# Channels 128 to 255 of both streams by taps summed in PSUM, b*s on GpSimd, a new bank plan, and W of f behind the projections

## The chip, the core and the metric

The kernel runs on one core of one Trainium2 chip. A core has five engines with a queue each: TensorE (PE in the profile; PEld is its weight load), VectorE (DVE), ScalarE (ACT), GpSimd (POOL) and SyncE (SP, which here only starts DMAs). They run side by side and wait for each other by semaphores. PE writes its results to PSUM, eight banks of 2 KB per partition, from where VectorE and ScalarE read them. The metric is the time of the whole program on the device in microseconds; the kernel before took 2464.41 us, the median of three runs (2457.53 to 2467.1).

## What is computed

A block of a vision network on `x` (4, 128, 96, 96): group normalisation, then a gated scan over the pixels in four directions (rows forward and backward, columns forward and backward), a fusing 1x1 convolution, and the residual.

```python
t = _grouped1x1(x, in_proj_w, in_proj_b, G)            # 4 groups
u, gate = (t[:, :HID], t[:, HID:])                     # 256 channels each
u = jax.nn.silu(u)
u = lax.conv_general_dilated(u, dw_w, ...)             # depthwise, K = 5
s = _conv1x1(u, ssm_in_w)                              # 32 channels
a = DMIN + (DMAX - DMIN) * jax.nn.sigmoid(_conv1x1(u, ssm_delta_w, ssm_delta_b))
a = jnp.clip(a, 0.0001, 0.9999)
bb = jnp.tanh(_conv1x1(u, ssm_b_w, ssm_b_b))
cc = jnp.tanh(_conv1x1(u, ssm_c_w, ssm_c_b))
prefix = jnp.cumsum(jnp.log(a), axis=-1)
hst = jnp.exp(prefix) * jnp.cumsum(bb * s * jnp.exp(-prefix), axis=-1)
u = u + _conv1x1(cc * hst + ssm_d[None, :, None] * s, ssm_out_w)
u = _grouped1x1(u * jax.nn.sigmoid(gate), mix_w, mix_b, G)
return _conv1x1(u, out_proj_w, out_proj_b)
...
seq_all = jnp.concatenate([seq_h, seq_h[:, :, ::-1], seq_v, seq_v[:, :, ::-1]], axis=0)
...
return jnp.einsum('oc,bchw->bohw', fuse_w, y) + fuse_b[None, :, None, None]
...
x = x + _L0_conv_ref(_gn(x), ...)
```

The recurrence behind `hst` is h = a * h + b * s, a scan over 9216 positions. mix, out_proj and fuse are linear and follow each other, so the kernel multiplies them into one matrix `w_fin` ("W") per direction at the start.

## The kernel before

**Tiling.** For each of four images there are two phases: the two column directions (order V), then the two row directions (order H). In a phase a forward stream f (s = 0) and a reversed stream r (s = 1) run together. A sequence is cut into 6 steps, and a step into 4 units by the position's remainder p modulo 4, each of N = 384 positions. A *unit* is one step, p and stream; a *pair* is the units of f and r with the same step and p. There are 192 pairs. `pair(t)` (line 507) is called for t = 0 to 198 and is a software pipeline: at call t the convolution and the projections are those of pair t, the inputs ("front") those of pair t + 4, and the gate, the sum and W ("back") those of pair t - 6 (LAG). So the first six calls have no back and the last seven no projections.

**Stages of a pair**, with the names used below:
- *rows* (line 323), twice a pair, the first and the second: 8 matmuls of 32x32 tiles for one front unit and 8 for the gate of one back unit; ScalarE takes the gate through tanh (`gv`) and the front through silu (`sil`), from four banks.
- *convolution* (`conv`, line 396): the depthwise convolution of a half of the channels of a unit as 8 matmuls with a band matrix, copied to `u` by ScalarE (line 402). Of the four halves of a pair (f and r, channels 0 to 127 and 128 to 255) three are done so. The fourth, channels 128 to 255 of f, is done by *taps* (line 407): one ScalarE operation for tap 0 and four VectorE operations that add tap k, on 384 elements in SBUF.
- *projections* (`proj`, line 422): 16 matmuls of `u` with `w_proj` into two banks, giving b and a in one, c and s in the other; ScalarE evacuates c and s. `inputs` (line 443), called in the next pair, evacuates b and a through tanh (line 447), brings a into its range on GpSimd (450, 451) and multiplies b by s on VectorE, straight from PSUM (452).
- *scan* (line 454): one VectorE scan over half a step, in the first two pairs of each step. *outputs* (line 469): three GpSimd operations that make c * h + d * s.
- *ssm_out* (line 381): 16 matmuls of 32x32 tiles into four banks; VectorE adds `u` to them and multiplies by the gate, once per stream (393, 394).
- *W of f, W of r* (`accumulate`, line 475): 8 matmuls with `w_fin` and one VectorE addition of the result y to the image `acc` (490, 495, 497). W of r is issued one pair later than W of f. In the last half of an H phase finished parts go out by DMA.

In phases V, VectorE also collects the statistics of the next image (`stats_chunk`, line 310).

**What sets the order.** The loop over `pair(t)` is recorded under a manual schedule: each of PE, VectorE, ScalarE and GpSimd runs its operations in the order of the calls in `pair`, and the framework adds the waits for data and for buffers, PSUM banks among them. The bank plan is thus a plan of waits:

```python
    GATE, FRONT, CONV_R, Y_F, SMALL = (0, 1), (2, 3), (0, 1), 2, 3
    SSM, PROJ, Y_R, CONV_F = (4, 6), (5, 4), 6, 7
```

On PE a pair is: first rows, W of r (of the pair before), convolution of f, second rows, ssm_out, two convolutions of r, W of f, projections. Every matmul but those of the preparation has line 314, that of the helper `mm`, and is told apart by its tiles: `psum<-x_in,wn` rows, `psum<-sil,band` convolution, `psum<-u,w_proj` projections, `psum<-t,w_so` ssm_out, `psum<-gv,w_fin` W. The profile counts two records for each matmul of fp32.

## Time and profile before

| | |
|---|---|
| median of three runs | 2464.41 us (2457.53 to 2467.1) |
| the profiled execution | 2462.79 us, span 2461.1 us |
| granted TensorE clock, mean | 0.992 |
| matmuls of rows, busy | 389.9 us |
| matmuls of ssm_out, busy | 256.2 us |
| matmuls of the projections, busy | 533.0 us |
| matmuls of W, busy | 582.9 us |
| VectorE waiting for PE ahead of L393 | 247.5 us, 133 times |
| ScalarE waiting for PE ahead of L402 | 339.3 us, 572 times |
| GpSimd waiting for ScalarE ahead of L450 | 1190.2 us, 189 times |

The span goes from the first to the last instruction. Busy times of a group count each moment once, though up to 16 small matmuls run at the same time. A row of the groups reads: line, engine, operation, what is written and what is read, shape and count, then busy us and the mean ns of one, then the idle time of the engine just before it and what ended that. A row of the timeline reads: start, length, engine, line, operation, and in brackets the idle time ahead of it.

### The profile page before, as it was taken

What the parts mean: (1) busy time and instruction counts of PE and PEld (TensorE: products, weight loads), DVE (VectorE), ACT (ScalarE), POOL (GpSimd) and SP (SyncE); (2) the same over time, 40 slices, a digit from 0 to 9 for tenths busy, and PEclk for the clock granted to TensorE, in tenths of its full rate; (3) what the DMA queues carried; (4) which work ended last, traced back from release to release, by engine and by line L of the source; (5) the groups of instructions that cost most, each with busy time, mean ns of one, the idle gap of its engine ahead of it and who ended that gap; (6) DMA issues with size and microseconds to landing.
All of it is one profiled execution on the core that took longest, in us unless ns stands there. A gap on an engine that the chain in (4) does not pass through costs nothing.

```text
span 2461.1 us, 89876 instructions
## 1 busy us (share of the span) xinstructions
PE 2389.1 (97%) x40016; PEld 913.3 (37%) x40016; DVE 1859.2 (76%) x2343; ACT 1572.8 (64%) x2912; POOL 1051.3 (43%) x1170
## 2 busy tenths in 40 slices
PE   6999999999999999999999999999999999999997
PEld 3333333333333333333333333333333333333331
DVE  3688777777887787777877788777777777777774
ACT  4666676666666666666665666666666666666641
POOL 4344444444444444444443444444443444444441
PEclk9999999999999999999999999999999999999997
DMA  5212111113332211111342211111232111111111
GB/s 140 56 47 54 47 41 32 38 31 89 98 100 52 54 44 34 35 38 31 93 139 55 54 46 41 31 38 31 52 120 89 31 38 33 38 31 38 25 45 56
DMA packets 79283, 134.21 MB, mean 55 GB/s; under 512 B 11440, under 2 KB 73392, under 8 KB 78896
## 3 DMA queue, kind: packets, MB, share of 16 engines
q1 hardware_dynamic: 76704, 127.64, 19.3%
q8 instruction: 314, 5.14, 0.9%
q10 hardware_dynamic: 2192, 0.83, 0.1%
q14 instruction: 73, 0.60, 0.1%
HBM read 109.55 MB, written 18.87 MB: 52 GB/s over the span
## 4 chain that ended last, share of the span: by engine, by line
PE 82%; DVE 9%; POOL 3%; ACT 3%; issue 1%; DMA 0%; DVEq 0%; SPq 0%
PE psum L314 82%; DVE t L465 4%; ACT t L447 2%; DVE gv L394 2%; DVE psum L393 2%; POOL t L450 1%; POOL t L451 1%; DVE u L415 0%; DMA out<-acc 0%; DVE bn L310 0%; DMA acc<-in_xr 0%; ACT gv L353 0%; ACT L364 0%; ACT L438 0%; ACT sil L364 0%
## 5 line engine op out<-in xcount | busy, mean ns | idle before, releaser
L314 PE MATMUL psum<-sil,band 128*32 128x384 f32 x9216 | 821.6, 488 | 0.0
L450 POOL TENSOR_SCALAR t<-t 64x384 f32<-64x384 f32 x192 | 186.3, 970 | 1190.4 <-ACT t L447 1190.2
L314 PE MATMUL psum<-gv,w_fin 128*32 128x384 f32 x6144 | 582.9, 497 | 31.0 <-DVE gv L394 29.0
L393 DVE TENSOR_TENSOR psum<-psum,u 128x768 f32<-128x768 f32 x384 | 369.3, 962 | 248.3 <-PE psum L314 247.5
L314 PE MATMUL psum<-u,w_proj 128*32 128x384 f32 x6144 | 533.0, 486 | 0.0
L415 DVE SCALAR_TENSOR_TENSOR u<-sil,w_tap,u 128x384 f32<-128x384 f32 x768 | 478.9, 624 | 56.9 <-ACT u L413 35.7
L353 ACT ACTIVATE gv<-psum,bnorm 128x384 f32<-128x384 f32 x768 | 403.7, 577 | 153.2 <-PE psum L314 153.2
L402 ACT COPY u<-psum 128x384 f32<-128x384 f32 x576 | 276.0, 479 | 339.3 <-PE psum L314 339.3
L314 PEld LDWEIGHTS psum<-sil,band 128*32 128x32 f32 x9216 | 284.0, 109 | 489.7 <-issue 344.9
L314 PE MATMUL psum<-x_in,wn 32*32 32x385 f32 (+1 forms) x12288 | 389.9, 502 | 13.3 <-DVE acc L490 8.5
L394 DVE SCALAR_TENSOR_TENSOR gv<-gv,psum 128x768 f32<-128x768 f32 x384 | 366.5, 955 | 43.7 <-ACT sil L364 0.9
L314 PEld LDWEIGHTS psum<-gv,w_fin 128*32 128x32 f32 x6144 | 183.5, 110 | 388.7 <-issue 289.6
L364 ACT ACTIVATE sil<-psum,bsilu 128x385 f32<-128x385 f32 x576 | 314.6, 586 | 5.6 <-PE psum L314 5.4
L438 ACT ACTIVATE t<-psum,b_proj 64x384 f32<-64x384 f32 x192 | 110.6, 576 | 321.7 <-PE psum L314 263.8
L314 PEld LDWEIGHTS psum<-u,w_proj 128*32 128x32 f32 x6144 | 211.9, 110 | 280.2 <-issue 276.6
L472 POOL TENSOR_TENSOR t<-t,t 64x384 f32<-64x384 f32 x192 | 289.1, 1506 | 15.0
L471 POOL TENSOR_TENSOR t<-t,t 64x384 f32<-64x384 f32 x192 | 249.5, 1300 | 95.9 <-DVE t L465 85.9
L314 PE MATMUL psum<-t,w_so 32*32 32x384 f32 x6144 | 256.2, 493 | 2.9 <-DVE t L452 2.9
L452 DVE TENSOR_TENSOR t<-psum,t 64x384 f32<-64x384 f32 x192 | 179.4, 934 | 103.9 <-ACT t L447 103.0
L447 ACT ACTIVATE t<-psum,b_proj 128x384 f32<-128x384 f32 x192 | 208.6, 1087 | 25.3 <-PE psum L314 2.3
L314 PEld LDWEIGHTS psum<-x_in,wn 32*32 32x32 f32 x12288 | 99.3, 104 | 275.3 <-ACT sil L364 129.9
L451 POOL TENSOR_SCALAR t<-t 64x384 f32<-64x384 f32 x192 | 184.9, 963 | 15.9
(62 smaller groups left out, 1166.5 us busy)
## 6 DMA issues: line engine op xcount, KB each, us to landing
x_in<-in_xs SPq DMA_DIRECT2D x96, 385.0 KB, 4.4
x_in<-in_xs SPq DMA_DIRECT2D x384, 96.2 KB, 2.6
out<-acc SPq DMA_DIRECT2D x24, 768.0 KB, 4.9
xs<-in_xr SPq DMA_DIRECT2D x72, 192.0 KB, 2.4
acc<-in_xr SPq DMA_DIRECT2D x18, 768.0 KB, 4.9
acc<-in_xr SPq DMA_DIRECT2D x24, 192.0 KB, 3.6
w_fuse<-in_fuse_wT ACTq DMA_DIRECT2D x1, 256.0 KB, 4.8
w_proj<-in_proj_wT ACTq DMA_DIRECT2D x1, 128.0 KB
```

Source lines behind the costliest of these rows:

```text
L314: nc.tensor.matmul(o[r, : rhs.shape[-1]], lhsT, rhs, start=start, stop=stop, skip_group_check=True)
L353: nc.scalar.activation(gv[:, j, :], bank(GATE[j])[:, :N], AF.Tanh, bias=gbn[:, 2 + j : 3 + j], scale=0.5,)
L364: nc.scalar.activation(sil[:, j, g, :], bank(front_banks[j])[:, : N + 1], AF.Silu, bias=bn[:, j : j + 1] if by_taps(s, j) else bsil[:, j, ...
L393: nc.vector.tensor_add(pz, pz, bu["u"])
L394: nc.vector.scalar_tensor_tensor(gv, gv, 1.0, pz, ALU.add, ALU.mult)
L402: nc.scalar.copy(un["u"][:, j, :], pc[:, :N])
L415: nc.vector.scalar_tensor_tensor(part, src, w_tap[:, k : k + 1], part, ALU.mult, ALU.add)
L447: nc.scalar.activation(ta[:, p, :], bank(PROJ[0])[:, :N], AF.Tanh, bias=b_proj[:, 0:1])
L450: nc.gpsimd.tensor_scalar(a, a, half, DMIN + half, ALU.mult, ALU.add)
L451: nc.gpsimd.tensor_scalar(a, a, 0.9999, 0.0001, ALU.min, ALU.max)
L471: nc.gpsimd.tensor_mul(ta[64:P, p, :], tb[0:64, p, :], ta[0:64, p, :])
L472: nc.gpsimd.tensor_add(tb[64:P, p, :], ta[64:P, p, :], tb[64:P, p, :])
```

## The change

Channels 128 to 255 are now done by taps for both streams. `u`, `sil` and the taps cover f and r in one operation of 2 x 384 elements; the partial sum stands in two PSUM banks (`TAPS`, 6 and 7), and only the last tap writes `u`. The band matrix keeps half of its columns. The addition of `u` behind ssm_out is one operation over four banks instead of two over two banks each. The four results of the projections are evacuated by ScalarE right behind them; s goes to a new tile `s` in SBUF, from where GpSimd multiplies b by it. `inputs` is gone. W of f stands behind the projections, taps 0 to 2 between the convolution of r and the projections, and taps 3 and 4 behind the first rows of the next pair. All banks are assigned anew: `rows` is told its banks (FIRST and SECOND), ssm_out uses 0 to 3, W of both streams bank 0, the convolutions 1 and 4, the projections 5 and 4.

On PE, between ssm_out and the next rows, the program before has (`sil_1` is the silu of stream r; `gv` goes into W; the rows of `w_proj` alternate 16 times between the two streams):

```order
L314 MATMUL psum<-t_18_10689,w_so 32x384 x16
L314 MATMUL psum<-sil_1_10861,band 32x384 x16
L314 MATMUL psum<-gv_0_1_0_11612,w_fin 32x384 x8
L314 MATMUL psum<-u_1_3_0_11568,w_proj 32x384
L314 MATMUL psum<-u_1_3_1_11682,w_proj 32x384
```

and the changed one, from the same place to the first rows (`x_in`) of the next pair, behind whose 16 alternating rows comes W of r:

```order
L315 MATMUL psum<-t_18_9965,w_so 32x384 x16
L315 MATMUL psum<-sil_9863,band 32x384 x8
L315 MATMUL psum<-u_1_3_0_10799,w_proj 32x384 x16
L315 MATMUL psum<-gv_0_1_0_10852,w_fin 32x384 x8
L315 MATMUL psum<-x_in_68,wn_3587 32x385
L315 MATMUL psum<-x_in_68,wn_3587 32x384
```

Eight of the 16 convolution matmuls are gone there, and W of f has moved behind the projections, next to the rows and W of r.

On VectorE, a pair with neither scan half, whose back is in a phase H and whose own convolution in a phase V (`bn` are statistics, `acc<-psum,b_fin` the y of f, `acc<-psum` that of r, `u` written from `sil` a tap), before:

```order
L495 SCALAR_TENSOR_TENSOR acc<-psum,b_fin,acc 128x16x24
L415 SCALAR_TENSOR_TENSOR u_0_2_0_14307<-sil_0_13458,w_tap,u_0_2_0_14307 128x384 x4
L452 TENSOR_TENSOR t_24_14163<-psum,t_24_14163 64x384
L497 TENSOR_TENSOR acc<-psum,acc 128x16x24
L310 BN_STATS bn_14085<-xs_2_14381 128x6
L393 TENSOR_TENSOR psum<-psum,u_5_0_0_13430 128x2x384
L394 SCALAR_TENSOR_TENSOR gv_5_0_0_14352<-gv_5_0_0_14352,psum 128x768
L393 TENSOR_TENSOR psum<-psum,u_5_0_1_13545 128x2x384
L394 SCALAR_TENSOR_TENSOR gv_5_0_1_14400<-gv_5_0_1_14400,psum 128x768
L495 SCALAR_TENSOR_TENSOR acc<-psum,b_fin,acc 128x16x24
```

and the changed one:

```order
L497 SCALAR_TENSOR_TENSOR acc<-psum,b_fin,acc 128x16x24
L419 SCALAR_TENSOR_TENSOR psum<-sil_12578,w_tap,psum 128x2x384
L419 SCALAR_TENSOR_TENSOR u_0_2_0_13361<-sil_12578,w_tap,psum 128x2x384
L499 TENSOR_TENSOR acc<-psum,acc 128x16x24
L311 BN_STATS bn_13170<-xs_2_13447 128x6
L387 TENSOR_TENSOR psum<-psum,u_5_0_0_12541 128x4x384
L389 SCALAR_TENSOR_TENSOR gv_5_0_0_13416<-gv_5_0_0_13416,psum 128x768
L389 SCALAR_TENSOR_TENSOR gv_5_0_1_13466<-gv_5_0_1_13466,psum 128x768
L419 SCALAR_TENSOR_TENSOR psum<-sil_12578,w_tap,psum 128x2x384 x2
L497 SCALAR_TENSOR_TENSOR acc<-psum,b_fin,acc 128x16x24
```

The product of L452 is gone, the four taps are split around the y of f, two behind the products with the gate and two ahead of the y of r, and the two adds of L393 are one (L387).

On ScalarE, the end of a pair and the start of the next (`t` are the tiles of the scan: the first holds b and a, the other c and d * s), before:

```order
L402 COPY u_1_2_1_18543<-psum 128x384 x2
L413 ACTIVATE u_1_3_0_18571<-sil_0_17561,w_tap 128x384
L438 ACTIVATE t_31_18291<-psum,b_proj 64x384
L441 ACTIVATE t_31_18291<-psum,d_sb 64x384
L447 ACTIVATE t_31_18290<-psum,b_proj 128x384
L353 ACTIVATE gv_0_1_0_18615<-psum,bnorm_10976 128x384 x2
```

and the changed one:

```order
L403 COPY u_4_3_0_12406<-psum 128x384
L417 ACTIVATE psum<-sil_12039,w_tap 128x2x384
L445 ACTIVATE t_22_12140<-psum,b_proj 128x384
L446 ACTIVATE t_22_12141<-psum,b_proj 64x384
L448 COPY s_12563<-psum 64x384
L449 ACTIVATE t_22_12141<-psum,d_sb 64x384
L349 ACTIVATE gv_3_2_0_12595<-psum,bnorm_3722 128x384 x2
```

The tanh of b and a (L447, now L445) is the first of the evacuations, the copy of s is new, and one convolution copy is gone.

The diff, without the preparation on the host and the parts that only follow the new shapes:

```diff
-    GATE, FRONT, CONV_R, Y_F, SMALL = (0, 1), (2, 3), (0, 1), 2, 3
-    SSM, PROJ, Y_R, CONV_F = (4, 6), (5, 4), 6, 7
+    FIRST = ((2, 3), (1, 5))
+    Y_R, CONV_F = 0, 1
+    SECOND = ((6, 7), (4, 5))
+    SSM = 0
+    CONV_R, PROJ, TAPS, Y_F, SMALL = 4, (5, 4), 6, 0, 5
...
-    band = wp.tile([P, 2, R, 2, 4, 32], F32, name="band")
+    band = wp.tile([P, R, 2, 4, 32], F32, name="band")
...
     sils = {}
 
-    def rows(i, bi, front_banks=FRONT):
+    def rows(i, bi, banks):
...
-            if g == 0:
-                sils[step, s] = wk.tile(
-                    [P, 2, 4, N + 1], F32, tag=f"sil{s}", name=f"sil_{step}_{s}"
-                )
-            sil = sils[step, s]
+            if k == 0:
+                sils[step] = wk.tile([P, 2, 2, 4, N + 1], F32, tag="sil", name=f"sil_{step}")
+            sil = sils[step][:, s]
...
                     r = slice(32 * j, 32 * j + 32)
-                    m, q = (c, g) if by_taps(s, j) else (g, c)
-                    mm(bank(front_banks[j]), c, wn[r, 32 * m : 32 * m + 32], x_in[s][r, q, :],
+                    m, q = (c, g) if j else (g, c)
+                    mm(bank(banks[0][j]), c, wn[r, 32 * m : 32 * m + 32], x_in[s][r, q, :],
                        True, True)
                 if bi is not None:
                     r = slice(64 + 32 * j, 96 + 32 * j)
-                    mm(bank(GATE[j]), c, gwn[r, 32 * c : 32 * c + 32],
+                    mm(bank(banks[1][j]), c, gwn[r, 32 * c : 32 * c + 32],
...
     def ssm_out(bi):
 
-        pair = units[bi], units[bi + 1]
+        pair = units[bi : bi + 2]
...
                     r = slice(64 * j + 32 * s, 64 * j + 32 * s + 32)
-                    mm(bank(SSM[s] + j), c, w_so[r, 128 * j + 32 * c : 128 * j + 32 * c + 32],
+                    mm(bank(SSM + 2 * s + j), c, w_so[r, 128 * j + 32 * c : 128 * j + 32 * c + 32],
                        z[r, p, :], True, True)
+        pz = psum[:, SSM : SSM + 4, :N]
+        nc.vector.tensor_add(pz, pz, us[bi].rearrange("p s j n -> p (s j) n"))
         for s, bu in enumerate(pair):
-            pz, gv = psum[:, SSM[s] : SSM[s] + 2, :N], bu["v"]
-            nc.vector.tensor_add(pz, pz, bu["u"])
-            nc.vector.scalar_tensor_tensor(gv, gv, 1.0, pz, ALU.add, ALU.mult)
-
-    def conv(un, j):
-        sil = sils[un["step"], un["s"]]
-        pc = bank(CONV_R[j] if un["s"] else CONV_F)
+            nc.vector.scalar_tensor_tensor(
+                bu["v"], bu["v"], 1.0, pz[:, 2 * s : 2 * s + 2, :], ALU.add, ALU.mult
+            )
+
+    us = {}
+
+    def conv(i, s):
+
+        un = units[i]
+        sil = sils[un["step"]][:, s]
+        pc = bank(CONV_R if s else CONV_F)
         for k in range(2):
             for g in range(4):
-                mm(pc, g, band[:, j, un["p"], k, g, :], sil[:, j, g, k : k + N], k == 0, k == 1)
-        nc.scalar.copy(un["u"][:, j, :], pc[:, :N])
-
-    def new_u(un):
-        un["u"] = wk.tile([P, 2, N], F32, tag="u", bufs=2 * LAG + 2, name=f"u_{un['id']}")
-
-    def taps(un, ks):
-        sil, j = sils[un["step"], un["s"]], 1
+                mm(pc, g, band[:, un["p"], k, g, :], sil[:, 0, g, k : k + N], k == 0, k == 1)
+        nc.scalar.copy(us[i][:, s, 0, :], pc[:, :N])
+
+    def new_u(i):
+        us[i] = wk.tile([P, 2, 2, N], F32, tag="u", bufs=LAG + 1, name=f"u_{units[i]['id']}")
+
+    def taps(i, ks):
+
+        un = units[i]
+        sil = sils[un["step"]][:, :, 1]
+        part = psum[:, TAPS : TAPS + 2, :N]
         for k in ks:
             off, q = divmod(un["p"] + k, R)
-            src, part = sil[:, j, q, off : off + N], un["u"][:, j, :]
+            src = sil[:, :, q, off : off + N]
             if k == 0:
                 nc.scalar.activation(part, src, AF.Copy, scale=w_tap[:, 0:1])
             else:
                 nc.vector.scalar_tensor_tensor(
-                    part, src, w_tap[:, k : k + 1], part, ALU.mult, ALU.add
+                    us[i][:, :, 1, :] if k == K - 1 else part,
+                    src,
+                    w_tap[:, k : k + 1],
+                    part,
+                    ALU.mult,
+                    ALU.add,
                 )
...
-    def proj(i, which):
-
-        un = units[i]
-        step, p = un["step"], un["p"]
+    def proj(i):
+
+        step, p = units[i]["step"], units[i]["p"]
...
-        pp = bank(PROJ[which])
-        cols = (qb, qb, qa, qa) if which == 0 else (qc, qc, qs, qs)
-        for j in range(2):
-            for c in range(4):
-                mm(pp, c, w_proj[:, j, cols[c]], units[i + c % 2]["u"][:, j, :], j == 0, j == 1)
-        if which == 1:
-            nc.scalar.activation(
-                tb[0:64, p, :], pp[0:64, :N], AF.Tanh, bias=b_proj[0:64, 1:2]
-            )
-            nc.scalar.activation(tb[64:P, p, :], pp[64:P, :N], AF.Copy, scale=d_sb[64:P, :])
-
-    def inputs(i):
-
-        un = units[i]
-        ta, p = scans[un["step"]][0], un["p"]
-        nc.scalar.activation(ta[:, p, :], bank(PROJ[0])[:, :N], AF.Tanh, bias=b_proj[:, 0:1])
+        for j in (1, 0):
+            for bk, cols in zip(PROJ, ((qb, qb, qa, qa), (qc, qc, qs, qs))):
+                for c in range(4):
+                    mm(bank(bk), c, w_proj[:, j, cols[c]], us[i][:, c % 2, j, :], j == 1, j == 0)
+        pa, pb = (bank(bk)[:, :N] for bk in PROJ)
+        nc.scalar.activation(ta[:, p, :], pa, AF.Tanh, bias=b_proj[:, 0:1])
+        nc.scalar.activation(tb[0:64, p, :], pb[0:64, :], AF.Tanh, bias=b_proj[0:64, 1:2])
+        st = wk.tile([P, N], F32, tag="s", name=f"s_{i}")
+        nc.scalar.copy(st[0:64, :], pb[64:P, :])
+        nc.scalar.activation(tb[64:P, p, :], pb[64:P, :], AF.Copy, scale=d_sb[64:P, :])
         a = ta[64:P, p, :]
         half = (DMAX - DMIN) / 2
         nc.gpsimd.tensor_scalar(a, a, half, DMIN + half, ALU.mult, ALU.add)
         nc.gpsimd.tensor_scalar(a, a, 0.9999, 0.0001, ALU.min, ALU.max)
-        nc.vector.tensor_mul(ta[0:64, p, :], bank(PROJ[1])[64:P, :N], ta[0:64, p, :])
...
         conv_here = i < NU
         front = i + UB if i + UB < NU else None
-        back = 0 <= bi < NU
-        if 0 <= i - 2 < NU:
-            inputs(i - 2)
-        rows(front, bi if back else None)
+        back = bi if 0 <= bi < NU else None
+        rows(front, back, FIRST)
+        if conv_here and i:
+            taps(i, range(3, K))
         if 0 <= bi - 2 < NU:
             accumulate(units[bi - 1])
         if conv_here:
-            conv(units[i], 0)
+            conv(i, 0)
         if k < 2 and 0 <= t // R - 1 < NU // UB:
             scan(t // R - 1, k)
...
-            rows(None if front is None else front + 1, bi + 1 if back else None)
-        if back:
+        if front is not None or back is not None:
+            rows(None if front is None else front + 1, None if back is None else bi + 1, SECOND)
+        if back is not None:
             ssm_out(bi)
         if conv_here:
-            new_u(units[i + 1])
-            for j in range(2):
-                conv(units[i + 1], j)
-        if back:
+            conv(i, 1)
+        if i + 2 < NU:
+            new_u(i + 2)
+            taps(i + 2, range(3))
+        if conv_here:
+            proj(i)
+        if back is not None:
             accumulate(units[bi])
         if later:
             next(later[0], None)
-        if i + 2 < NU:
-            new_u(units[i + 2])
-            taps(units[i + 2], range(K))
-        if conv_here:
-            proj(i, 1)
-            proj(i, 0)
 
     for _ in stats_finish(b0):
         pass
     for i in range(UB):
-        rows(i, None, (2 * (i % 2), 2 * (i % 2) + 1))
-    new_u(units[0])
-    taps(units[0], range(K))
+        rows(i, None, (SECOND[0] if i % 2 else FIRST[0], None))
+    new_u(0)
```

43 lines of the change are left out of this document (20 added, 23 removed).

## The prediction

> **The bound.** I read the page first: the busy shares and the chain that ended last.
>
> ```profile
> PE 2389.1 (97%) x40016; PEld 913.3 (37%) x40016; DVE 1859.2 (76%) x2343; ACT 1572.8 (64%) x2912; POOL 1051.3 (43%) x1170
> PE 82%; DVE 9%; POOL 3%; ACT 3%; issue 1%; DMA 0%; DVEq 0%; SPq 0%
> ```
>
> TensorE is busy 97% of the span and carries 82% of the chain; the next engine, VectorE, is at 76%. Busy shares are averages, so the second view is the table by stage. I cut it where the first pair with all its stages begins (t = 6) and where the last pair with projections ends; 186 pairs lie between.
>
> ```profile
> 100.24:2392.06 2291.82, 2261.64 (x38565) 862.76 (x38562) 1781.08 (x2228) 1507.13 (x2786) 991.98 (x1038) 1.00 0.20 52
> ...
> 2394.00:2419.00 25.00, 16.18 (x248) 4.73 (x240) 16.95 (x18) 5.40 (x11) 15.61 (x16) 0.86 0.22 79
> 2419.00:2461.00 42.00, 30.18 (x320) 8.16 (x320) 17.90 (x23) 6.31 (x12) 1.43 (x2) 0.68 0.10 39
> ```
>
> The columns are the stretch, its length, then busy time on PE, PEld, DVE, ACT and POOL, and the granted clock (the third number from the end). A pair takes 2291.82 / 186 = 12.32 us, PE is busy 98.7% of it at a clock of 1.00, and 2461.1 - 2291.8 = 169.3 us lie outside. So a pair of the middle decides, and the third view is the timeline of one in which nothing waits:
>
> ```profile
> 1147.53 0.94 PE L314 MATMUL psum<-x_in,wn 32*32 32x385 f32 x32
> 1148.40 1.50 PE L314 MATMUL psum<-gv,w_fin 128*32 128x384 f32 x16
> 1149.72 1.48 PE L314 MATMUL psum<-sil,band 128*32 128x384 f32 x16
> 1151.12 0.94 PE L314 MATMUL psum<-x_in,wn 32*32 32x385 f32 x32
> 1151.79 1.30 PE L314 MATMUL psum<-t,w_so 32*32 32x384 f32 x32
> 1153.03 2.79 PE L314 MATMUL psum<-sil,band 128*32 128x384 f32 x32
> 1155.63 1.48 PE L314 MATMUL psum<-gv,w_fin 128*32 128x384 f32 x16
> 1156.92 2.77 PE L314 MATMUL psum<-u,w_proj 128*32 128x384 f32 x32
> 1159.62 0.94 PE L314 MATMUL psum<-x_in,wn 32*32 32x385 f32 x32
> ```
>
> Starts are in the first column. From start to start: first rows 0.87, W of r 1.32, convolution of f 1.40, second rows 0.67, ssm_out 1.24, convolutions of r 2.60, W of f 1.29, projections 2.70; together 12.09. The mean of 12.32 is these steps plus 0.23 of waits. VectorE in the same pair:
>
> ```profile
> 1149.97 0.56 DVE L497 TENSOR_TENSOR acc<-psum,acc 128x384 f32<-128x384 f32 x1 [0.23 <-PE psum L314]
> 1153.05 0.97 DVE L393 TENSOR_TENSOR psum<-psum,u 128x768 f32<-128x768 f32 x1 [2.53 <-PE psum L314]
> 1154.13 0.95 DVE L394 SCALAR_TENSOR_TENSOR gv<-gv,psum 128x768 f32<-128x768 f32 x1
> 1155.00 0.96 DVE L393 TENSOR_TENSOR psum<-psum,u 128x768 f32<-128x768 f32 x1
> 1156.07 0.95 DVE L394 SCALAR_TENSOR_TENSOR gv<-gv,psum 128x768 f32<-128x768 f32 x1
> 1157.25 0.62 DVE L495 SCALAR_TENSOR_TENSOR acc<-psum,b_fin,acc 128x384 f32<-128x384 f32 x1 [0.23 <-PE psum L314]
> ```
>
> VectorE waits for PE here, not the reverse. The rows also give the latencies I need: an add of y starts 1.57 after W of r starts and 1.62 after W of f; the add behind ssm_out starts 1.26 after ssm_out; an operation that needs the result before it starts 0.11 after its end (1153.05 + 0.97, then 1154.13), and one that doesn't starts 0.87 after the start of one of 768 elements.
>
> **TensorE.**
>
> ```profile
> L314 PE MATMUL psum<-sil,band 128*32 128x384 f32 x9216 | 821.6, 488 | 0.0
> ```
>
> Three convolutions a pair become two. Of the 2.60 for the two of r one half goes: 1.30 a pair (a third of the group's 821.6 us is 274; 192 x 1.30 = 250). The other steps stay, in another order, so PE's steps are 12.09 - 1.30 = 10.79. That alone would be 186 x 10.79 + 169 = 2176 us; what follows is what is late next.
>
> **New banks.** Three places now share a bank that did not before, and each wait is a small sum of rows.
>
> ```profile
> 1151.26 0.48 ACT L402 COPY u<-psum 128x384 f32<-128x384 f32 x1 [0.59 <-PE psum L314]
> ```
>
> ```profile
> 1118.27 0.95 DVE L394 SCALAR_TENSOR_TENSOR gv<-gv,psum 128x768 f32<-128x768 f32 x1
> ```
>
> ```profile
> 1119.37 1.50 PE L314 MATMUL psum<-gv,w_fin 128*32 128x384 f32 x16 [0.27 <-DVE gv L394]
> ```
>
> The copy out of a convolution starts 1.54 after it (1149.72, 1151.26) and takes 0.48; PE starts 0.15 after the release (1119.22, 1119.37).
> - W of f and, in the next pair, W of r both use bank 0. W of r needs the add of f's y done: 1.62 + 0.62 + 0.15 = 2.39 after W of f starts. PE gets there after 1.40 + 0.87 = 2.27 (W of f now stands ahead of rows, like the convolution with its 1.40). Wait: 0.12. Behind it stand on PE the convolution of f and all else of the pair.
> - ssm_out writes bank 1, from which f's convolution is copied: 1.54 + 0.48 + 0.15 = 2.17 against 1.40 + 0.67. Wait: 0.10.
> - The projections write bank 4, from which r's convolution is copied, after one quarter of their work in bank 5: 2.17 against 1.30 + 0.64. Wait: 0.23.
>
> Together 0.45, so 11.24 a pair, if VectorE keeps up.
>
> **VectorE.** Its operations and their durations:
>
> ```profile
> L415 DVE SCALAR_TENSOR_TENSOR u<-sil,w_tap,u 128x384 f32<-128x384 f32 x768 | 478.9, 624 | 56.9 <-ACT u L413 35.7 <-ACT sil L364 1.0
> L393 DVE TENSOR_TENSOR psum<-psum,u 128x768 f32<-128x768 f32 x384 | 369.3, 962 | 248.3 <-PE psum L314 247.5
> L394 DVE SCALAR_TENSOR_TENSOR gv<-gv,psum 128x768 f32<-128x768 f32 x384 | 366.5, 955 | 43.7 <-ACT sil L364 0.9 <-ACT u L402 0.5
> L452 DVE TENSOR_TENSOR t<-psum,t 64x384 f32<-64x384 f32 x192 | 179.4, 934 | 103.9 <-ACT t L447 103.0
> L465 DVE TENSOR_TENSOR_SCAN t<-t,t 64x768 f32<-64x768 f32 x40 | 116.8, 2919 | 14.9 <-POOL t L451 14.9
> L465 DVE TENSOR_TENSOR_SCAN t<-t 64x768 f32<-64x768 f32 x56 | 107.4, 1918 | 5.2 <-POOL t L451 3.6
> ```
>
> Four taps of 384 elements become four of 768, with the sum in PSUM. The trace has no such tap. It can't be shorter than the 384 form (0.62) nor should it pass two of them (1.25); the nearest row is L394, the same operation on 768 elements with one operand in PSUM: I take 0.96. The two adds of L393 become one of 1536: between 0.97 and 1.92; the step from L497 (0.56 at 384) to L393 (0.96 at 768) is 0.40 per 384, so 0.96 + 0.81 = 1.77. The product of L452 (0.93) goes to GpSimd. A pair therefore gains 4 x 0.96 + 1.77 - 4 x 0.62 - 2 x 0.96 - 0.93 = 0.28 on VectorE: 9.7 (1859.2 / 192) becomes 10.0, of 11.2. The sum fits; the order is the question, because f's y, which now gates bank 0, stands behind two taps. From the start of ssm_out: 1.26, the add 1.77, 0.11, two products at 0.87, the first of two taps 1.07 (0.96 + 0.11) and the second 0.88, so VectorE is free for f's add at 6.83. It is due at 1.24 + 1.30 + 0.23 + 2.58 (projections: twice the 1.29 of W of f, whose operations are half as many) + 1.62 = 6.97. That is a slack of 0.14, so no wait in a pair without a scan.
>
> The scan stands between the add of r's y and the add behind ssm_out, in two pairs of four. Before it come f's add, taps three and four and r's add. F's add starts 1.62 after W of f, the third tap 0.53 later (0.09 before its end, as above), the fourth 1.07, r's add 0.87: 4.09, which is 1.70 after W of r (2.39), where r's y alone would let it start after 1.57. The first scan (2.92 in 40 of 48 steps) then ends at 1.70 + 0.47 + 2.92 = 5.09 after W of r; the add behind ssm_out is due at 1.32 + 1.40 + 0.67 + 0.10 + 1.26 = 4.75. Late by 0.34, less the slack: 0.20. The second (1.92) ends by 4.09, in time.
>
> ```profile
> L310 DVE BATCH_NORM_STATS2 bn<-xs 128x6 f32<-128x384 f32 x72 | 39.9, 555 | 1.1
> ```
>
> In 72 of 192 pairs L310 adds 0.47 there: 0.67 in such a first scan pair; the second still ends by 4.56. Over four pairs 0.62 x 0.20 + 0.38 x 0.67 = 0.38, that is 0.09 a pair: 11.33 a pair.
>
> **Other engines.** ScalarE loses one convolution copy (0.48), gains a copy of s (0.48), and its tap of 384 (0.62) becomes one of 768, at most 1.24: from 8.2 (1572.8 / 192) to 8.8 of 11.33. Its chain behind r's convolution, 1.24 + 1.54 + 0.48 + 1.24 = 4.50 after ssm_out starts, is done before VectorE comes to the first tap (1.26 + 1.77 + 0.11 + 0.87 + 0.87 = 4.88), even at that bound.
>
> ```profile
> L471 POOL TENSOR_TENSOR t<-t,t 64x384 f32<-64x384 f32 x192 | 249.5, 1300 | 95.9 <-DVE t L465 85.9
> L450 POOL TENSOR_SCALAR t<-t 64x384 f32<-64x384 f32 x192 | 186.3, 970 | 1190.4 <-ACT t L447 1190.2
> L451 POOL TENSOR_SCALAR t<-t 64x384 f32<-64x384 f32 x192 | 184.9, 963 | 15.9
> ```
>
> ```profile
> L447 ACT ACTIVATE t<-psum,b_proj 128x384 f32<-128x384 f32 x192 | 208.6, 1087 | 25.3 <-PE psum L314 2.3
> ```
>
> GpSimd's b*s is like L471 (one strided operand, strided result): 1.30, between the 0.96 of L451, with one operand, and two of L471; so 5.5 (1051.3 / 192) becomes 6.8. What it could hold up is the first scan. The tanh of L447 now comes right behind the projections and ends about 0.6 after W of f starts; then 0.97 + 0.96 + 1.30 and three gaps of some 0.1 make 4.1. The scan's turn on VectorE is at 2.39 + 1.70 + 0.47 = 4.6. Hidden, with 0.5 to spare; beyond that each first scan goes later by the excess, at 2.60 by 0.8, which is 0.2 a pair or 37 us.
>
> **Outside.** Outside the 186 pairs, the first six pairs save at most 6 x 1.30; I take 2, because taps in one PSUM region form a chain from pair to pair that no other work covers there. In the last seven, W of f waits for the sum of both streams, 0.81 longer: +5.6. At the start 32 of 64 band operations on GpSimd go, beside the loads and statistics: 0. `stats_finish` runs three times in the middle, with its matmuls behind W of f as before: 0. The DMAs stay where they were, in `rows` and W; they come 8% closer together, at a DMA share of 0.20 (second column from the end of the stage's row).
>
> **The sum.** 186 x 11.33 = 2107; + 169.3 - 2 + 5.6 = 2280 of span. The profiled execution took 2462.8 with a span of 2461.1, and the median of the three runs is 1.6 above it: 2284 us.
>
> **A rule.** This view belongs to the end of the program, where PE waits in every pair:
>
> ```profile
> 2419.26 1.54 PE L314 MATMUL psum<-gv,w_fin 128*32 128x384 f32 x16 [2.06 <-DVE gv L394]
> 2420.73 1.53 PE L314 MATMUL psum<-x_in,wn 32*32 32x384 f32 x16
> 2422.19 2.79 PE L314 MATMUL psum<-gv,w_fin 128*32 128x384 f32 x16
> ```
>
> The same 16 matmuls take 1.54 and then 2.79, and the stage's clock is 0.68. So waits of 2 us in each pair do cost clock; the new ones are 0.1 to 0.7. The Trainium skill ("TensorE: Matmul & The Clock Gate", section "A second HAM failure mode: psum-queue depth-cycling") says that a kernel which cycles PSUM banks each iteration idles briefly between groups often enough for the clock to swing between half and full. By its two rates, evenly mixed, the estimate would be 10.79 / 0.75 + 0.54 a pair, 2953 us in all; the trace speaks against that here, since the 1.3% of idle time in the middle stage left the clock at 1.00.
>
> **The rivals.**
> - VectorE becomes the bound, because a tap costs two of the old ones (1.25). For: a per-column scalar, two SBUF segments and a PSUM target in one operation are in no row. Against: L393 and L394 touch PSUM at 768 and stay at 0.96. Taps one and two then add 0.58 between ssm_out and f's add, 0.44 beyond the slack, in every pair; taps three and four add 0.58 in each first scan pair, 0.15 a pair: 11.92, and 2393 us. An add of 1.92 instead of 1.77 is worth at most a quarter of that.
> - The new waits don't show, because copies and adds start sooner than these rows: 10.79 a pair and 2183 us; a tap of 0.62 gives 11.24 and 2267.
> - Slower than before: PE's clock falls through the new gaps. Place: the three bank waits and f's add, four gaps a pair. Price: at the 0.86 of the window 2394 to 2419, 10.79 / 0.86 + 0.54 = 13.1 a pair, 2611 us. It decides once the granted clock of the middle stage is below 0.92, where 10.79 / 0.92 + 0.54 = 12.3 is what a pair takes now. Against it: the wait of 0.27 in the row at 1119.37 stands in the middle stage already, at 1.00.
>
> **The numbers.** Forecast (2240 to 2335) 0.70; VectorE as the bound (2335 to 2440) 0.18; waits hidden (2180 to 2240) 0.07; clock (slower than before) 0.05. The range 2225 to 2395 takes the first, over half of the second and some of the third: 0.82. The chance of faster by over 0.5%, about what a measurement can tell from no change, is 0.94; of slower 0.05; the 0.01 between is a partial loss of clock.
>
> **The test.** A pair of 11.2 to 11.4 in the table by stage at a clock of 1.00; matmuls from sil and band at two thirds of their count; W of r (psum<-gv,w_fin) waiting for the add of f's y by 0.1, and by 0.3 to 0.9 in first scan pairs; the projections waiting for the copy of u by 0.2; taps at 0.96 and the add of 1536 at 1.77 in the groups; the product on GpSimd at 1.3. Wrong would be: taps at 1.1 or more, a scan that waits for GpSimd's product, PE waiting at the second rows for tap four (it would be 0.8 late to do so), or a clock below 0.99.

## The result, and the profile after

The changed kernel takes 2255.13 us, the median of 4 runs (2253.9 to 2258.31), against 2465.52 (2457.53 to 2467.1) of the kernel before on the same chip: a ratio of 0.9155, 95% interval 0.9132 to 0.9177. The profiled execution took 2253.9 us, span 2252.2.

From the page after, the busy shares and the shares of the chain that ended last:

```profile
PE 2171.5 (96%) x36944; PEld 775.2 (34%) x36944; DVE 1881.1 (84%) x1959; ACT 1583.0 (70%) x2912; POOL 1279.4 (57%) x1330
PE 75%; DVE 18%; DMA 2%; ACT 2%; issue 1%; SPq 0%; DVEq 0%; ACTq 0%
```

TensorE lost 218 us of busy time and the span 209. VectorE's share of the chain doubled, from 9% to 18%. The table by stage, cut at the same pairs as before (columns as in the prediction):

```profile
97.81:2182.14 2084.33, 2054.67 (x35590) 733.70 (x35586) 1798.92 (x1856) 1517.90 (x2788) 1226.43 (x1227) 1.00 0.22 57
2184.00:2208.00 24.00, 15.74 (x248) 3.84 (x240) 14.50 (x14) 5.47 (x11) 14.18 (x14) 0.86 0.18 63
2208.00:2252.00 44.00, 26.51 (x320) 6.46 (x320) 18.86 (x20) 6.32 (x12) 2.23 (x3) 0.80 0.12 48
```

A pair of the middle takes 2084.33 / 186 = 11.21 us at a clock of 1.00; 167.9 us lie outside. The groups that carry the change:

```profile
L315 PE MATMUL psum<-sil,band 128*32 128x384 f32 x6144 | 575.5, 492 | 1.1 <-ACT gv L349 1.1
L419 DVE SCALAR_TENSOR_TENSOR psum<-sil,w_tap,psum 128x768 f32<-128x768 f32 x576 | 586.3, 1018 | 36.7 <-ACT psum L417 29.7
L387 DVE TENSOR_TENSOR psum<-psum,u 128x1536 f32<-128x1536 f32 x192 | 338.9, 1765 | 240.3 <-PE psum L315 216.5
L454 POOL TENSOR_TENSOR t<-s,t 64x384 f32<-64x384 f32 x192 | 238.6, 1243 | 14.5
L467 DVE TENSOR_TENSOR_SCAN t<-t,t 64x768 f32<-64x768 f32 x40 | 91.4, 2285 | 1.3
```

Two thirds of the convolution's matmuls are left. A tap of 768 elements takes 1.02, the sum of 1536 1.77, GpSimd's b*s 1.24. The first scan fell from 2.92 to 2.29 though it wasn't touched (the section on the hardware comes back to it). And the timeline of TensorE and of VectorE over one pair without a scan, from ssm_out to the next ssm_out:

```profile
1132.68 1.28 PE L315 MATMUL psum<-t,w_so 32*32 32x384 f32 x32
1133.89 1.50 PE L315 MATMUL psum<-sil,band 128*32 128x384 f32 x16
1135.20 2.92 PE L315 MATMUL psum<-u,w_proj 128*32 128x384 f32 x32
1137.94 1.47 PE L315 MATMUL psum<-gv,w_fin 128*32 128x384 f32 x16
1139.35 0.94 PE L315 MATMUL psum<-x_in,wn 32*32 32x385 f32 x32
1140.24 1.50 PE L315 MATMUL psum<-gv,w_fin 128*32 128x384 f32 x16
1141.55 1.47 PE L315 MATMUL psum<-sil,band 128*32 128x384 f32 x16
1142.96 0.94 PE L315 MATMUL psum<-x_in,wn 32*32 32x385 f32 x32
1143.63 1.30 PE L315 MATMUL psum<-t,w_so 32*32 32x384 f32 x32
```

```profile
1134.05 1.77 DVE L387 TENSOR_TENSOR psum<-psum,u 128x1536 f32<-128x1536 f32 x1 [1.90 <-PE psum L315]
1135.85 1.82 DVE L389 SCALAR_TENSOR_TENSOR gv<-gv,psum 128x768 f32<-128x768 f32 x2
1137.59 2.08 DVE L419 SCALAR_TENSOR_TENSOR psum<-sil,w_tap,psum 128x768 f32<-128x768 f32 x2
1139.57 0.61 DVE L497 SCALAR_TENSOR_TENSOR acc<-psum,b_fin,acc 128x384 f32<-128x384 f32 x1
```

The pair takes 10.95. Its projections take 2.74 from start to start where 2.58 was worked out: a wait of 0.16 inside them, at bank 4. VectorE goes from the sum to the add of f's y without a gap; that add ends at 1140.18 and W of r starts at 1140.24. So two chains have the same length: TensorE's steps with the wait at bank 4, and a loop from ssm_out over VectorE to W of r (7.56) and from there back to ssm_out (3.39), 10.95.

The rest of the 11.21 stands in few pairs. Pair lengths, from the start of one projections to the next, sorted by what the pair holds, as the excess over the median of the pairs without any of it (the median is rounded to 0.01, so an excess over the 92 scan pairs is good to some 0.5 us):

| us | before | after | last variant (below) |
|---|---|---|---|
| median of the other pairs | 12.07 | 10.95 | 10.80 |
| pairs at a first or second scan, excess in all | 25.0 | 7.7 | 5.8 |
| nine pairs at `stats_finish` | 7.2 | 15.0 | 16.5 |
| three pairs at the change of the image | 15.0 | 24.0 | 1.3 |
| the stage in all | 2291.8 | 2084.3 | 2034.3 |
| outside it | 169.3 | 167.9 | 169.1 |

One of the three, in the timeline of TensorE (first row) and VectorE (second), and the clock of two stretches of the same place (the third number from the end):

```profile
648.28 2.79 PE L315 MATMUL psum<-gv,w_fin 128*32 128x384 f32 x16 [4.17 <-DVE acc L492]
647.66 0.56 DVE L492 TENSOR_TENSOR acc<-psum,acc 128x384 f32<-128x384 f32 x1 [4.18 <-DMA acc<-in_xr]
...
648.00:650.80 2.80, 2.52 (x16) 0.79 (x20) 2.17 (x3) 0.00 (x0) 0.72 (x2) 0.50 0.00 0
650.80:653.50 2.70, 2.70 (x20) 0.59 (x12) 1.02 (x2) 0.00 (x0) 0.00 (x0) 0.50 0.08 15
```

The first add of a new image needs all of it in `acc`; its last part is loaded behind the DMA that writes the finished part out. W of r waits 4.17 for that, and the next two steps run at half the clock, 1.3 longer each. All of the stage's half clock stands at these three places, 17 us in the trace.

### The profile page after: what moved, and what is told of

Read it like the earlier page. It is cut to its first block, busy times and chain, and to the rows that moved or that the text cites. A ratio compares the mean times of both kernels' runs of the same rounds, so it can differ in the third digit from the quotient of the medians.

```text
span 2252.2 us, 82167 instructions
## 1 busy us (share of the span) xinstructions
PE 2171.5 (96%) x36944; PEld 775.2 (34%) x36944; DVE 1881.1 (84%) x1959; ACT 1583.0 (70%) x2912; POOL 1279.4 (57%) x1330
## 4 chain that ended last, share of the span: by engine, by line
PE 75%; DVE 18%; DMA 2%; ACT 2%; issue 1%; SPq 0%; DVEq 0%; ACTq 0%
PE psum L315 75%; DVE psum L419 5%; DVE psum L387 4%; DVE gv L389 4%; DVE t L467 2%; DMA out<-acc 1%; DVE u L419 1%; DVE acc L492 1%; ACT gv L349 0%; DVE bn L311 0%; DMA acc<-in_xr 0%; DVE acc L497 0%; ACT psum L417 0%; ACT sil L360 0%; DMA x_in<-in_xs 0%
## 5 line engine op out<-in xcount | busy, mean ns | idle before, releaser
L419 DVE SCALAR_TENSOR_TENSOR psum<-sil,w_tap,psum 128x768 f32<-128x768 f32 x576 | 586.3, 1018 | 36.7 <-ACT psum L417 29.7
L315 PE MATMUL psum<-sil,band 128*32 128x384 f32 x6144 | 575.5, 492 | 1.1 <-ACT gv L349 1.1
L452 POOL TENSOR_SCALAR t<-t 64x384 f32<-64x384 f32 x192 | 182.6, 951 | 684.6 <-ACT t L445 684.5
L387 DVE TENSOR_TENSOR psum<-psum,u 128x1536 f32<-128x1536 f32 x192 | 338.9, 1765 | 240.3 <-PE psum L315 216.5
L403 ACT COPY u<-psum 128x384 f32<-128x384 f32 x384 | 184.1, 479 | 233.8 <-PE psum L315 233.8
L445 ACT ACTIVATE t<-psum,b_proj 128x384 f32<-128x384 f32 x192 | 191.9, 999 | 158.8 <-PE psum L315 125.4
L315 PEld LDWEIGHTS psum<-sil,band 128*32 128x32 f32 x6144 | 181.1, 110 | 348.3 <-issue 198.1
L315 PEld LDWEIGHTS psum<-u,w_proj 128*32 128x32 f32 x6144 | 180.3, 109 | 346.8 <-issue 221.9
L454 POOL TENSOR_TENSOR t<-s,t 64x384 f32<-64x384 f32 x192 | 238.6, 1243 | 14.5
L360 ACT ACTIVATE sil<-psum,bsilu 128x385 f32<-128x385 f32 x384 | 224.4, 584 | 7.8 <-PE psum L315 7.3
L360 ACT ACTIVATE sil<-psum,bnorm 128x385 f32<-128x385 f32 x384 | 227.1, 591 | 0.0
L419 DVE SCALAR_TENSOR_TENSOR u<-sil,w_tap,psum 128x768 f32<-128x768 f32 x192 | 194.9, 1015 | 6.7
## 6 DMA issues: line engine op xcount, KB each, us to landing
xs<-in_xr SPq DMA_DIRECT2D x72, 192.0 KB, 2.4
acc<-in_xr SPq DMA_DIRECT2D x24, 192.0 KB, 3.6
```

The lines of the kernel that those rows point to most:

```text
L315: nc.tensor.matmul(o[r, : rhs.shape[-1]], lhsT, rhs, start=start, stop=stop, skip_group_check=True)
L360: nc.scalar.activation(sil[:, j, g, :], bank(banks[0][j])[:, : N + 1], AF.Silu, bias=bn[:, 1:2] if j else bsil[:, g : g + 1],)
L387: nc.vector.tensor_add(pz, pz, us[bi].rearrange("p s j n -> p (s j) n"))
L403: nc.scalar.copy(us[i][:, s, 0, :], pc[:, :N])
L419: nc.vector.scalar_tensor_tensor(us[i][:, :, 1, :] if k == K - 1 else part, src, w_tap[:, k : k + 1], part, ALU.mult, ALU.add,)
L445: nc.scalar.activation(ta[:, p, :], pa, AF.Tanh, bias=b_proj[:, 0:1])
```

## Experiments

Each kernel ran beside the kernel before; its ratio is to that. "Pair" is the median of the pairs without a scan, an image change or `stats_finish`; stage and outside are of the profiled span.

| kernel | median us (range) | ratio, 95% interval | pair | stage | outside |
|---|---|---|---|---|---|
| the change | 2255.1 (2253.9 to 2258.3) | 0.9132 to 0.9177 | 10.95 | 2084.3 | 167.9 |
| conv_r_twice | 2488.2 (2487.4 to 2490.8) | 1.008 to 1.012 | 12.22 | 2305.8 | 179.9 |
| taps_sbuf | 2459.1 (2450.5 to 2465.4) | 0.9964 to 0.9996 | 11.68 | 2288.9 | 170.2 |
| bs_vector | 2386.1 (2383.3 to 2387.7) | 0.9663 to 0.9708 | 11.81 | 2207.5 | 173.8 |
| w_f_ahead | 2690.0 (2687.2 to 2695.3) | 1.0894 to 1.0944 | 12.94 | 2512.7 | 173.4 |
| add_by_stream | 2268.9 (2268.1 to 2271.7) | 0.9199 to 0.923 | 11.13 | 2098.5 | 167.8 |
| taps_by_stream | 2262.5 (2261.3 to 2263.5) | 0.9171 to 0.9201 | 11.06 | 2092.1 | 169.6 |
| wr_bank4 | 2259.6 (2254.3 to 2265.0) | 0.9153 to 0.9197 | 10.94 | 2075.9 | 176.6 |
| conv_r_bank6 | 2258.9 (2255.8 to 2261.6) | 0.9148 to 0.9189 | 10.97 | 2078.5 | 180.4 |
| both_banks | 2248.7 (2246.8 to 2251.5) | 0.9109 to 0.915 | 10.80 | 2055.1 | 192.0 |
| out_tile | 2234.8 (2232.9 to 2235.9) | 0.9055 to 0.9087 | 10.95 | 2061.7 | 171.6 |
| banks_and_out | 2223.7 (2219.9 to 2226.8) | 0.9006 to 0.9046 | 10.80 | 2038.6 | 185.7 |
| banks_and_out_ends | 2207.8 (2205.1 to 2211.2) | 0.8951 to 0.8978 | 10.80 | 2034.3 | 169.1 |

### What the parts of the change are worth

**conv_r_twice.**

```diff
-        for k in range(2):
+        for k in [0, 1] * times:          # times = 2 for r, else 1
             for g in range(4):
                 mm(pc, g, band...
```

> The 8 matmuls of r's convolution are issued twice with the same result, so TensorE has the work it had before the change (three convolutions a pair) and all else is as changed. Theory A, the whole gain is the convolution that left TensorE: a pair goes from 10.95 by 1.30 to 12.25, the waits of first scan pairs (about 11 us in all) go under; 2255 + 192 x 1.30 - 11 = 2494 us, so the other edits by themselves cost some 30 us against the 2465 of before. Rival B, the new order and banks bring a part of the gain by themselves: below 2450 us. Rival C, half of the 1.30 is hidden behind VectorE: about 2375 us.

2488 us, and 12.22 a pair: theory A. With the old amount of work on TensorE the new plan is some 1% slower than the old one, so the gain is the convolution that left TensorE. The other edits bring nothing by themselves; taps_sbuf, bs_vector and w_f_ahead show what the gain loses without three of them.

**taps_sbuf.**

```diff
-        part = psum[:, TAPS : TAPS + 2, :N]
+        part = parts[i]               # wk.tile([P, 2, N]), one for each pair
```

> The partial sum of the taps stands in SBUF and not in PSUM; both streams still in one operation. Theory A: a tap of 768 elements takes as long with all operands in SBUF, 1.02 us, and the time stays at 2255 us within 0.5%. Rival B, the PSUM operand makes a tap longer: at 0.95 two taps ahead of the add of f's y save 0.14 a pair, at most 26 us. Rival C, operands in SBUF collide with GpSimd, as the first scan does (2.31 us beside a GpSimd product of 2.49, 1.81 alone): taps at 1.2 to 1.5, 0.4 to 1.0 a pair later, 2330 to 2440 us.

2459 us: nearly the whole gain is gone, the worst case of C and a little beyond. Part of it is clock: 51 us of the trace's stage run at 0.50, against 17 in the changed kernel. The groups of its taps on VectorE and of b*s on GpSimd:

```profile
L422 DVE SCALAR_TENSOR_TENSOR part<-sil,w_tap,part 128x768 f32<-128x768 f32 x576 | 737.5, 1280 | 30.4 <-ACT part L420 23.2
L422 DVE SCALAR_TENSOR_TENSOR u<-sil,w_tap,part 128x768 f32<-128x768 f32 x192 | 324.6, 1690 | 6.8
...
L457 POOL TENSOR_TENSOR t<-s,t 64x384 f32<-64x384 f32 x192 | 341.7, 1779 | 14.5
```

and the same taps one by one (min/median/max ns), which holds the answer:

```profile
L422 DVE SCALAR_TENSOR_TENSOR part<-sil,w_tap,part x576: 949/1134/1890, 44.9 to 2374.0; 128x768 f32<-128x768 f32 x192
L422 DVE SCALAR_TENSOR_TENSOR u<-sil,w_tap,part x192: 1017/1855/1911, 48.2 to 2375.1; 128x768 f32<-128x768 f32 x192
```

The fastest tap in SBUF takes as long as one in PSUM (949 and 952 ns); in PSUM none takes over 1024. What differs is the neighbour: GpSimd's product next to these taps grew from 1.24 to 1.78 as well. The Trainium skill ("GPSIMD Engine Reference", section "1. Specifications") says that GpSimd shares its SBUF interfaces with VectorE and contends with VectorE instructions that have two SBUF inputs. The rows agree: the tap with both inputs in SBUF and GpSimd's product lengthen together, and with one of the inputs in PSUM neither does. Taken singly, the 248 taps of up to 1.06 us in this trace have GpSimd working beside them for 23% of their time, the 342 of 1.5 us and more for 91%; in the changed kernel it is 68%, and no tap is longer for it.

**bs_vector.**

```diff
-        nc.gpsimd.tensor_mul(ta[0:64, p, :], st[0:64, :], ta[0:64, p, :])
...
+        nc.vector.tensor_mul(b_p, s_p, b_p)      # in the next pair, behind tap four
```

> b*s runs on VectorE again (from the tile s in SBUF, between tap four and the add of r's y), all else as changed. Theory A, VectorE's order is the second bound although it is busy 84%: 0.93 us more ahead of each scan makes the sum behind ssm_out later by about 0.93 in the first and 0.4 to 0.9 in the second scan pair, and W of r with it; pairs without a scan have room (the add of r's y ends 2.35 after W of r starts, ssm_out comes at 3.39). 48 x (1.4 to 1.8) = 67 to 87 us: 2322 to 2342. Rival B, VectorE has room everywhere: 2255 us. Rival C, it costs in every pair: 2255 + 186 x 0.93 = 2428 us.

2386 us, 44 above the upper end of A and 42 below C. By the pairs it is C's picture: against the changed kernel the cost shows in most pairs, those without a scan included, 0.86 at their median, because the product with both inputs in SBUF isn't the 0.93 of the old one from PSUM:

```profile
L520 DVE TENSOR_TENSOR t<-s,t 64x384 f32<-64x384 f32 x192 | 278.9, 1452 | 0.0
```

Single ones take 0.86 to 2.10. What A and C share (VectorE's order binds at 84% busy) holds and B falls; A's room in pairs without a scan was not there for 1.45.

**w_f_ahead.**

```diff
-        if conv_here:
-            proj(i)
         if back is not None:
             accumulate(units[bi])
+        if conv_here:
+            proj(i)
```

> W of f stands ahead of the projections again, all else as changed. Theory A: W of f needs the first product with the gate, which ends 1.37 + 1.80 + 0.95 + 0.05 = 4.17 us after ssm_out starts, and TensorE is there at 1.21 + 1.32 = 2.53; it waits 1.64 in each pair, the wait of 0.15 at bank 4 goes: 10.95 + 1.49 = 12.44 a pair, 2255 + 186 x 1.49 = 2532 us at a clock of 1.00. Rival B: a wait of 1.64 in every pair also costs clock; at the 0.86 of the first window of the tail, 10.79 / 0.86 + 1.64 = 14.2 a pair and 2860 us. Rival C, the place of W of f is without effect: 2255 us.

2690 us, between A and B. The timeline of TensorE in a pair without a scan:

```profile
2002.95 1.50 PE L315 MATMUL psum<-sil,band 128*32 128x384 f32 x16
2005.92 1.50 PE L315 MATMUL psum<-gv,w_fin 128*32 128x384 f32 x16 [1.48 <-DVE gv L389]
2007.24 2.76 PE L315 MATMUL psum<-u,w_proj 128*32 128x384 f32 x32
2009.93 1.43 PE L315 MATMUL psum<-x_in,wn 32*32 32x385 f32 x32
2011.29 1.50 PE L315 MATMUL psum<-gv,w_fin 128*32 128x384 f32 x16
```

W of f starts 2.97 after the convolution of r, 1.65 later than its 1.32: A's wait. What A missed is the next row pair: the first rows take 1.36 instead of 0.89, because bank 5, which holds b and a, goes to the gate of the first rows, and with W of f no longer in between its evacuation isn't done. 12.44 + 0.47 is the 12.91 to 12.94 measured. The rest of the time is in scan pairs, some 83 us, and B has a share in it. The granted clock of the pair above is 1.00, and none of the 142 waits of about 1.5 in the stage was followed by a lower one. In first scan pairs the wait is longer, and then the clock does fall:

```profile
1978.31 2.54 PE L315 MATMUL psum<-gv,w_fin 128*32 128x384 f32 x16 [2.23 <-DVE gv L389]
...
1978.60:1981.90 3.30, 3.30 (x26) 1.11 (x22) 3.27 (x5) 0.00 (x0) 0.00 (x0) 0.50 0.00 0
```

The stage has 30 such stretches of 3.4 us at 0.50, each behind a wait of 1.8 to 2.7; they are what makes its mean clock 0.98. At half the clock TensorE loses half of its busy time in them, up to 50 us by my estimate.

**add_by_stream** and **taps_by_stream**: one operation over both streams, taken apart.

```diff
-        nc.vector.tensor_add(pz, pz, us[bi].rearrange("p s j n -> p (s j) n"))
         for s, bu in enumerate(pair):
+            nc.vector.tensor_add(pz[:, 2 * s : 2 * s + 2, :], ..., us[bi][:, s])
```

> The sum behind ssm_out is taken in two operations of 768 again, each followed by its product with the gate; all else as changed. Theory A, a loop through VectorE (ssm_out, sum, products, taps one and two, add of f's y, bank 0, W of r, convolution of f, rows, ssm_out) takes 7.55 + 3.39 = 10.94 us, as long as the pair, so what it gains shows in full: from the first sum to the first tap 3.02 + 0.87 instead of 2.68 + 0.87, 0.34 a pair, 186 x 0.34 = 63 us and 2318 us. Rival B, VectorE has the slack of 0.14 that the prediction gave it: 0.20 a pair, 2292 us. Rival C, it has more: 2255 us.

```diff
-                nc.vector.scalar_tensor_tensor(..., src, ..., part, ...)
+                for s in range(2):
+                    nc.vector.scalar_tensor_tensor(..., src[:, s], ..., part[:, s], ...)
```

> Each tap is two VectorE operations of 384 elements, one for each stream; the sum stays in PSUM, tap zero in one ScalarE operation. Theory A, two independent operations of 384 follow each other at 0.53 us, so a tap takes 1.06 where one of 768 takes 1.05 from start to start: 2255 us within 0.5%. Rival B, each operation costs its full 0.62: 0.2 more a tap, two of them ahead of the add of f's y in a loop without slack, 0.4 a pair and 2330 us.

Pairs of 11.13 and 11.06: 0.18 and 0.11 more, 33 and 20 us over 186 pairs. The totals rose by 14 and 7 only, since the waits at the image change came out at 7.5 and 12.1 instead of 24.0 in these runs. So the total alone would have pointed to C for the first (14 us off, where B is 23 off) and A for the second; by the pairs the first is B's size and the second lies between its theories, nearer to A.

### What binds the pair now

**wr_bank4** and **conv_r_bank6**, and **both_banks**, which has both edits:

```diff
-    Y_R, CONV_F = 0, 1
+    Y_R, CONV_F = 4, 1
```

> W of r writes bank 4 instead of bank 0, so it no longer waits for the add of f's y; all else as changed. Theory A, the loop through bank 0 is what makes first scan pairs longer (0.35 in 22 of phase V, 0.15 in 24 of phase H); with it cut, the next to bind is the second rows, which wait for the add of r's y (bank 4), in the first scan pair by 0.1: 2255 - 8 = 2247 us; other pairs stay at 10.95, since bank 4 holds the projections there. Rival B, W of r now waits for the evacuation of c and s (it ends 0.2 before W of r in the trace) or the second rows for the add of r's y in every pair: 2260 us or more. Rival C, the waits of scan pairs have another cause: 2255 us.

```diff
-    CONV_R, PROJ, TAPS, Y_F, SMALL = 4, (5, 4), 6, 0, 5
+    CONV_R, PROJ, TAPS, Y_F, SMALL = 6, (5, 4), 6, 0, 5
...
+        first = banks is SECOND
+        if i is not None and first:
+            silu()                                    # ahead of the gate's tanh
```

> The convolution of r writes bank 6 instead of bank 4, and the front units' silu of the second rows goes ahead of the gate's tanh on ScalarE so that bank 6 is free in time; the projections then don't wait 0.15 for the copy of the convolution. Theory A, the loop of 10.94 us through VectorE and bank 0 binds as well, so the pair stays at 10.94: 2252 us. Rival B, the wait at bank 4 alone stands between the pair and its steps: 10.80 a pair, 2255 - 28 = 2227 us. Rival C, the convolution of r now waits for silu, or the product for the later tanh: 2270 us or more.

> W of r in bank 4 and the convolution of r in bank 6 together (with silu ahead of tanh in the second rows). Each alone left pairs without a scan at 10.91 to 10.93. Theory A, two chains of the same length bind, the projections' wait at bank 4 on TensorE and the loop through VectorE and bank 0, and only both edits shorten the pair: to the steps, 10.79 to 10.82, so 186 x 0.13 = 24 us less, and some 5 us less in first scan pairs: 2226 us. Rival B, a third chain binds at 10.9, VectorE's own order up to the add of r's y ahead of the second rows: 2250 us. The waits for the image's load at the image change (t = 55, 103, 151; 24 us in the changed kernel's trace, 8 to 24 in the others) come on top in either case and differ from run to run.

Each edit alone leaves the pair at 10.94 and 10.97; both together bring it to 10.80. That is what two chains of one length do, and A said so. In conv_r_bank6 the wait is seen to move:

```profile
1972.26 2.76 PE L315 MATMUL psum<-u,w_proj 128*32 128x384 f32 x32
1974.84 1.47 PE L315 MATMUL psum<-gv,w_fin 128*32 128x384 f32 x16
1976.24 0.94 PE L315 MATMUL psum<-x_in,wn 32*32 32x385 f32 x32
1977.24 1.50 PE L315 MATMUL psum<-gv,w_fin 128*32 128x384 f32 x16
```

The projections are down to 2.58, and W of r now starts 1.00 behind the first rows instead of 0.89: what bank 4 gave, bank 0 takes. The excess of scan pairs fell from 7.7 to about 4 in wr_bank4, but to about 2 in conv_r_bank6, which leaves the loop through bank 0 as it is; so these traces don't show that this loop alone makes them longer. The totals missed: 2260 us in wr_bank4, where A gave 2247, 2259 in conv_r_bank6 for 2252, and 2249 for both, where 2226 was expected. The stage got 29 us shorter, but the time outside went from 168 to 192. In the first six pairs, which have no back, the convolution of r waits for silu; in the last seven the second rows wait for the add of r's y (0.68 in the trace of banks_and_out), at a lower clock.

### The image change

**out_tile**, **banks_and_out** (with both_banks) and **banks_and_out_ends** (new banks only where a pair has both a back and projections):

```diff
+        dst = fin[s][:, :, p, :] if bu["st"] >= NS // 2 else part
...
-            nc.sync.dma_start(out[b, :, r], accf[:, r])
             if b + 1 < B:
                 nc.sync.dma_start(accf[:, r], xr[b + 1, :, r])
+            nc.sync.dma_start(out[b, :, r], fin[s].rearrange("p h r m -> p (h r m)"))
```

> In the second half of a phase H the sum of y and the image goes to a tile of its own, from which the DMA to the output reads; so the load of the next image into acc starts at once and not behind that DMA. All else as changed. Theory A, the 24 us at the three image changes (pairs of 17.9, 20.9 and 18.0 instead of 10.95) are this wait for the image plus the half clock behind it: these pairs fall to 11 to 12, 2255 - 22 = 2233 us. Rival B, the load itself is late (the queue or the bandwidth, not the order): 2250 us or more.

> The edits of both_banks and out_tile together: if they act at different places the gains add, 2255 - 29 - 22 = 2204 us; if the shorter pair brings the next image's first add nearer to its load, some of it comes back, up to 10 us: 2214 us.

```diff
-        py = bank(Y_R if s else Y_F)
+        py = bank(y_r if s else Y_F)      # y_r is bank 0 in the last seven pairs
...
-            conv(i, 1)
+            conv(i, 1, 4 if back is None else CONV_R)
```

> As banks_and_out, but the new banks only where they help: in the first six pairs, which have no back, the convolution of r stays in bank 4, and in the last seven W of r stays in bank 0. Theory A, what the middle stage gained (10.96 a pair against 11.21) was partly given back at the ends: 104.5 us before t = 6 instead of 97.8, since the convolution of r waits for silu there, and 81.3 us of tail instead of 72.8 (out_tile), since the second rows wait 0.7 for the add of r's y and the clock is lower; both come back: 2224 - 6.7 - 8.5 = 2208 us. Rival B, the ends were longer because of the chip's clock and not of the banks: 2224 us.

out_tile: 2235 us, and the excess at the image change falls from 24.0 to 1.6, as A said. banks_and_out missed by 20 us for the ends; with them mended, 2208 us is what A gave. It beats both kernels, at 0.8965 of before (0.8951 to 0.8978), and its stage has a pair of 10.94:

```profile
96.06:2130.33 2034.27, 2028.61 (x35590) 760.28 (x35586) 1790.81 (x1856) 1534.62 (x2788) 1227.14 (x1227) 1.00 0.22 59
```

TensorE is busy 99.7% of it. What remains beside its steps is mostly `stats_finish`, 16.5 us in nine pairs (the busy share shows only part of such a wait, since it counts a group of matmuls that is held up inside as busy). About half of it is in three of the nine, where the Sqrt on ScalarE and three table loads of 1.28 stand between silu and tanh in the trace; taking them away was not tried on the chip.

## Why the forecast was near, step by step

- **The convolution.** The steps were to be 10.79 without any wait; 10.95 less the 0.16 in the projections is 10.79, and with both waits removed the pair is 10.80. This term was right to a hundredth, and conv_r_twice shows that it carries the gain.
- **New banks: the term that was mis-sized.** I took 0.12 + 0.10 + 0.23 = 0.45. Measured: 0.02 at bank 0, nothing at bank 1 (ssm_out follows the second rows by 0.67), 0.16 at bank 4: 0.18, or 50 us less. The 0.15 from a release to TensorE's start, taken from a single row, was too long: 1140.18 to 1140.24 is 0.06.
- **VectorE.** The taps were put at 0.96 from the row with one input in PSUM and came out at 1.02; the sum at 1.77 was exact. Its add of f's y was to come at 6.83 behind ssm_out and comes at 6.89. The slack of 0.14 shrank to nothing, since that add was due sooner than I had it; add_by_stream shows that a delay there reaches the pair. The rival of a dear tap (1.25) was off for this kernel, but the row chosen was right for a reason that I didn't give: beside GpSimd it is the input in PSUM that keeps a tap at 1.02.
- **Scan pairs.** I carried the first scan over at 2.92 and had 17 us for it. It took 2.29, and these pairs cost 7.7.
- **Left out: `stats_finish` and the image change.** I put the first at nothing and had no term for the second, although both stand in the 0.23 of waits that I read off the middle stage of before. They cost 39.0 us after (22.2 before).
- **Ends.** The start was right (-2.4 for -2); the tail grew by 1.0 and not by 5.6, at a clock of 0.80 in its second window against 0.68.
- **The rule on the clock.** No loss from the new waits: 1.00 in the middle stage, and in w_f_ahead none behind waits of 1.5, so the rival that ended slower has no support at waits of 0.02 to 0.16. The rule itself, that waits of 2 us cost clock, held: in w_f_ahead those of 1.8 to 2.7 did in 30 of 46 cases.

In sum: the bank waits, the scans and the tail were 64 us too high and the two left out 39 us too low, which leaves 25 of the 29 us between forecast and measurement. Its closeness owes something to errors of opposite sign.

## What to carry to other kernels

When work moves from the bounding engine to the next one, look for the loop that runs through both: two chains of the same length hide each other, and only an edit of both shows what either costs. Carry over into a forecast every wait of the old profile that the change doesn't touch, by place, and not only the steps. And judge a bank edit by the stage it is meant for and by the ends apart, since a plan that fits the full pair can cost more in pairs where a neighbour is missing.
